# Result weighting, dense stores, result buffers and the pair rate of the last batches in a two-layer graph-attention and mixture-of-experts kernel

## The chip, the cores and the metric

The kernel runs on one core of one Trainium2 chip. The metric is the device time of one execution in microseconds (us), from the first to the last instruction with what lies around it; the median of several runs is compared. TensorE is called PE (its weight loads PEld), VectorE DVE, ScalarE ACT, GpSimd POOL, and SP is the engine that only issues transfers. Each engine works through its own list of instructions in order.

## The reference, cut to what matters

There are 64 batches of 256 tokens with 256 numbers each. Two layers of graph attention and feed-forward work follow each other; the second feed-forward is a mixture of 8 experts, of which each token uses two:

```
x = x + elu(attention of 4 heads over layernorm(x), masked by adj)
x = x + layernorm(x) @ weight.T + bias
x = x + relu(attention of 1 head over layernorm(x), masked by adj)
tokens = layernorm(x)
probs = softmax(tokens @ router_w.T); two largest per token, weights made to sum to 1
out = tokens
for e in range(8):
    h = gelu(tokens @ w1[e] + b1[e]); y = h @ w2[e] + b2[e]
    out = out + combine[:, e] * y
x = x + out
```

## The kernel before

A batch goes through `batch_layers` (L466): four attention heads, the feed-forward layer, one attention head, then the normalised tokens `xng` and the start of the result, `base`. For the first 62 batches `base` is stored to `out` straight away (L563), and the expert part is done by routing. Batches are routed in chunks: 12 chunks of four batches, six of two, two of one. `route` (L860) finds the two experts of each token, works out the row of each in a list in memory, and sends the tokens' rows there with indirect transfers from POOL (`send`, L843).

256 rows of one expert are a **pair** (two blocks of 128). `expert_pair` (L686) loads a pair's rows (`xr`, L701) and its expert's first weights (`we`, L712) from SP's queue, transposes the rows on PE (`px`, L719), copies them on ACT (`sT`, L723), makes the row numbers `to` and the weights `w` on DVE (L726 to L732), multiplies (`ph`, L751), applies gelu on ACT (`hT`, L757), multiplies again (`py`, L766), adds the bias on DVE into a result buffer `y` (L772), and weights `y` by `w` on ACT (L744). `scatter` (L777) then adds the 256 rows to `out` by two indirect transfers with addition from POOL (L783). Every such transfer is made to wait until those of the pair before have landed, so all scatters form one chain. There are 131 pairs, each with two scatter transfers; 14 of them, the partly filled ones, can start only when the last routed batch has been sent.

The last two batches are **dense**: `dense_expert` (L797) runs all eight experts over them, adds into `base` on DVE (L809), and stores `base` at the end (L816) through SP's queue. That gives 16 dense jobs.

The order of all instructions is written by a hand-made scheduler (`while more or active ...`, L1002). Time is cut into *steps*, three steps are a *period*, and a batch starts in each period (at steps 2, 5, 8, ... 191). Every job is a generator; each step runs every active job up to its next `yield`, in the order of the number it yielded before, its *rank*. A low rank comes early in the step. This is the only order there is: an instruction of rank 60 stands behind one of rank 2 in the list of each engine that has both. At the last step of each period pairs are started from a list named `waiting`, as many as a credit allows:

```
if phase == 2:
    credit = min(credit + (2.0 if more else 3.0), 3.0)
    while waiting and credit >= 1.0:
        credit -= 1.0
        begin(waiting.pop(0)(), 90)
```

`more` is true as long as batches are still to be started, up to step 191. A pair that starts at step s issues `xr` at s (rank 90), `we` at s+1 (rank 90), `px`, `sT`, `to` and `w` at s+2 (rank 60), `ph` and `hT` at s+3 (rank 30), `py` and the bias at s+4 (rank 80), and the weighting at s+5 (rank 2). Step s+5 is the same kind of step as s+2, so the weighting of one period's pairs and the row copies `sT` of the next period's pairs are in the same step. Scatters are started one per step at most, at rank 97, from step s+6 on. A dense job issues its `we` load one step, its `ph` three steps and its `py` four steps after it starts; with the eighth job of a batch the store follows at once, ahead of the `we` loads (rank 90) of the same step.

Tiles of one name take turns in a fixed number of buffers: `y` 7, `xr` 5, `we` 7, `z` (the attention probabilities) 6, `me` 2, `to` and `w` 8. PE's outputs share 8 banks.

Of the kernel before, what the change touches and what calls it, by code (L numbers as in the profile page):

```python
# [9 lines left out]
F32 = mybir.dt.float32  # L10
I32 = mybir.dt.int32
# [4 lines left out]
P = 128  # L16
# [11 lines left out]
def kernel(  # L28
# [18 lines left out]
    B, N, D = x.shape  # L47
# [4 lines left out]
    NT = N // P  # L52
# [17 lines left out]
    TICKS = 3  # L70
# [3 lines left out]
    work = ctx.enter_context(tc.tile_pool(name="work", bufs=2))  # L74
# [47 lines left out]
    mhalf = const.tile([P, 2 * NT], F32, tag="mhalf", name="mhalf")  # L122
    nc.vector.memset(mhalf, -0.5)

    adj_i = work.tile([P, NT, N], adj.dtype, tag="z", name="adj_i", bufs=6)
    nc.scalar.dma_start(out=adj_i, in_=adj.rearrange("(t p) j -> p t j", p=P))

    masks = [
# [100 lines left out]


    C_B1, WROW = KT * D, KT * D + 64
    WBUFS, XBUFS, YBUFS = 7, 5, 7
    wpack = tc.dram_tile([E, P, WROW], F32, name="wpack")
    w2s = const.tile([P, E, KT * D], F32, tag="w2s", name="w2s")
    b2s = const.tile([P, E, D], F32, tag="b2s", name="b2s")
# [157 lines left out]
    def projected1(xT, rstd, b):  # L393

        q = q1s[b % 2]
        pqs = []
        for t in range(NT):
            pq = bank("pq", [D + 3])
            for k in range(KT):
                nc.tensor.matmul(  # L400
                    pq, xT[:, k, t * P : (t + 1) * P], wx1[:, k, :],
                    start=(k == 0), stop=(k == KT - 1),
                )
            pqs.append(pq)
        ex = small.tile([P, NT, 3], F32, tag="ex1", name="ex1")
        for t, pq in enumerate(pqs):
            nc.scalar.activation(ex[:, t, :], pq[:, D:], AF.Exp, scale=rstd[:, t : t + 1])
            nc.scalar.activation(
                q[:, t, :D], pq[:, :D], AF.Copy, scale=rstd[:, t : t + 1]
            )  # L410
        me = work.tile([P, NT, N], F32, tag="me", name="me")
        for j in range(NT):
            nc.scalar.activation(me[:, j, :], masks[1][:, j, :], AF.Copy, scale=ex[:, j, 0:1])
        return q, ex, me

    def scores1(ex, me):
        pd = bank("pd", [N])
        for t in range(NT):
            nc.tensor.transpose(
                pd[:, t * P : (t + 1) * P], ex[:, t, 1:2].to_broadcast([P, P]), ident  # L420
            )
        z = work.tile([P, NT, N], F32, tag="z", name="z", bufs=6)
        for j in range(NT):
            nc.vector.scalar_tensor_tensor(
                z[:, j, :], pd, ex[:, j, 2:3], me[:, j, :], op0=ALU.max, op1=ALU.mult
            )
        return z

    def scores(q, heads, hs, mask, probs):

        d = D // heads
        pd = bank("pd", [len(hs), N])
        for i, h in enumerate(hs):
            for t in range(NT):
                nc.tensor.transpose(  # L435
                    pd[:, i, t * P : (t + 1) * P],
                    q[:, t, h, d + 1 : d + 2].to_broadcast([P, P]), ident,
                )
        for i, h in enumerate(hs):
            z = work.tile([P, NT, N], F32, tag="z", name="z", bufs=6)  # L440
            for j in range(NT):
                nc.vector.scalar_tensor_tensor(  # L442
                    z[:, j, :], pd[:, i, :], q[:, j, h, d + 2 : d + 3], mask[:, j, :],
                    op0=ALU.max, op1=ALU.mult,
                )
            probs.append(z)
# [239 lines left out]
    def expert_pair(j, n, ids, ef, regs, needs):  # L686

        i = j % GROUP
        upto = min(j + GROUP, n)
        if i == 0:  # L690
            _, regs["e"] = nc.values_load_multi_w_load_instructions(
                ids[0:1, 0, j:upto], engines=[mybir.EngineType.SP], min_val=0, max_val=E - 1,
                skip_runtime_bounds_check_because=WHY,
            )
            _, regs["t"] = nc.values_load_multi_w_load_instructions(
                ids[0:1, 1, j:upto], engines=[mybir.EngineType.SP], min_val=0, max_val=E * CAP,
                skip_runtime_bounds_check_because=WHY,
            )
        e_sp, t_sp = regs["e"][i], regs["t"][i]
        xr = io.tile([P, 2, ROW], F32, tag="xr", name="xr", bufs=XBUFS)  # L700
        load = nc.sync.dma_start(  # L701
            out=xr,
            in_=xs_d.rearrange("(t p k) c -> t p k c", p=P, k=2)[
                bass.ds(t_sp, 1), :, :, :
            ].rearrange("t p k c -> (t p) k c"),
        )
        tc.add_to_no_dep_group("rows", load.ins)
        for name in needs:
            tc.add_manual_dep(load.ins, name, AFTER, reason="any sent row may lie in the pair")
        yield 90  # L710
        we = io.tile([P, WROW], F32, tag="we", name="we", bufs=WBUFS)
        nc.sync.dma_start(  # L712
            out=we, in_=wpack[bass.ds(e_sp, 1), :, :].rearrange("e p c -> (e p) c")
        )
        yield 60
        px = bank("px", [KT, PAIR])
        for t in range(2):
            for k in range(KT):
                nc.tensor.transpose(  # L719
                    px[:, k, t * P : (t + 1) * P], xr[:, t, k * P : (k + 1) * P], ident  # L720
                )
        xT = work.tile([P, KT, PAIR], F32, tag="sT", name="sT", bufs=3)
        nc.scalar.copy(xT, px)  # L723

        to = small.tile([P, 2], I32, tag="to", name="to", bufs=8)
        nc.vector.tensor_copy(to[:, :, None], xr[:, :, D : D + 1])  # L726
        w = small.tile([P, 2], F32, tag="w", name="w", bufs=8)
        nc.vector.scalar_tensor_tensor(  # L728
            w[:, :, None], xr[:, :, D + 1 : D + 2], ef[:, j : j + 1], xr[:, :, D + 2 : D + 3],
            op0=ALU.is_equal, op1=ALU.mult,  # L730
        )
        nc.vector.tensor_tensor(w[:, :, None], w[:, :, None], xr[:, :, D + 3 : D + 4], ALU.add)  # L732
        yield 30
        hT = hidden(xT, we)
        yield 80
        if i == 0:
            _, regs["x"] = nc.values_load_multi_w_load_instructions(
                ids[0:1, 0, j:upto], engines=[mybir.EngineType.PE, mybir.EngineType.DVE],
                min_val=0, max_val=E - 1, skip_runtime_bounds_check_because=WHY,
            )  # L740
        y = result(hT, bass.ds(regs["x"][i], 1))
        yield 2
        for t in range(2):
            nc.scalar.activation(y[:, t, :], y[:, t, :], AF.Copy, scale=w[:, t : t + 1])  # L744
        scatters.append((y, to))
# [51 lines left out]
    def dense_expert(b, e):  # L797

        own = dense_batch[b]
        yield 90  # L800
        we = io.tile([P, WROW], F32, tag="we", name="we", bufs=WBUFS)
        nc.sync.dma_start(out=we, in_=wpack[e])
        yield 40
        yield 30
        hT = hidden(own["xT"], we)
        yield 80
        y = result(hT, slice(e, e + 1))
        for t in range(NT):
            nc.vector.scalar_tensor_tensor(  # L809
                own["base"][:, t, :], y[:, t, :], own["w"][:, t, e : e + 1],  # L810
                own["base"][:, t, :], op0=ALU.mult, op1=ALU.add,
            )
        if e == E - 1:
            while b == B - 1 and (scatters or len(added) < 2 * PAIRS):
                yield 99
            d = nc.sync.dma_start(  # L816
                out=out_rows[b * N : (b + 1) * N, :].rearrange("(t p) d -> p t d", p=P),
                in_=own["base"],
            )
            before = added[-2:] + based if b == B - 1 else []  # L820
            tc.declare_no_dep(
                d.ins, query=SYNC, group="out", keep=before,
                reason="no row is added to here, or every add is in their chain",
            )
            for ins in before:
                tc.add_manual_dep(d.ins, ins.name, AFTER, reason="filling rows were added here")
            tc.add_to_no_dep_group("out", d.ins)
            nc.sync.nop()
# [168 lines left out]

    batches = jobs()
    step, more, credit = 2, True, 0.0
    SETUP_AT = 3  # L1000
    with tc.manual_schedule():
        while more or active or waiting or dense_jobs or scatters:  # L1002
# [6 lines left out]
            if step >= SETUP_AT and setup:  # L1009
                begin(setup.pop(0)(), 90)  # L1010
            if phase == 2:
                credit = min(credit + (2.0 if more else 3.0), 3.0)
                while waiting and credit >= 1.0:
                    credit -= 1.0
                    begin(waiting.pop(0)(), 90)
                for _ in range(2):
                    if dense_jobs:
                        begin(dense_jobs.pop(0)(), 90)
# [54 lines left out]
```

## Time and profile before

| What | Value |
|---|---|
| Median of 3 runs | 1713.54 us (1712.98 to 1722.15) |
| The profiled execution: its own time | 1715.78 us |
| Its span, first to last instruction | 1714.1 us |
| PE busy | 1550.8 us, 90% of the span |
| DVE busy | 1276.3 us, 74% |
| ACT busy | 897.4 us, 52% |
| POOL busy | 875.9 us, 51% |
| Mean granted PE clock | 0.958 of full |

A line of the profile's fifth part gives: source line, engine, operation, output and inputs, count, busy time and mean of one in ns, and then the idle time of the engine just before these instructions with what ended most of it. In a timeline a line gives start, duration, engine, line, and in square brackets the idle time before it. POOL's time for an indirect transfer is that of issuing it; when it has landed is seen from what waits for it.

### The profile page before, as it was taken

How to read it: one execution, taken by the hardware profiler on the slowest of the kernel's cores; microseconds unless marked ns; L12 is line 12 of the kernel's file. 1: busy time of each engine (PE TensorE's matmuls, PEld its weight loads, DVE VectorE, ACT ScalarE, POOL GpSimd, SP SyncE). 2: the span in 40 equal slices, each digit the busy share in tenths (PEclk: the TensorE clock that was granted, in tenths of full speed). 3: DMA queues.
4: the chain of work that ended last, by engine and by line, in shares of the span. 5: the costliest groups of instructions: out<-in, count | busy, mean ns of one | idle time of the engine just before them, and what ended most of it. 6: DMA issues, size and time to landing. Idle time of an engine off the chain costs nothing. (4 is left out here: it accounts for less than half of the span.)

```text
span 1714.1 us, 29732 instructions
## 1 busy us (share of the span) xinstructions
PE 1550.8 (90%) x8998; PEld 1366.5 (80%) x8998; DVE 1276.3 (74%) x4744; ACT 897.4 (52%) x1965; POOL 875.9 (51%) x790
## 2 busy tenths in 40 slices
PE   5899889899999999999999999999999998797792
PEld 4777778788888888898888888888889887676681
DVE  5889998978787888878787878788788977522221
ACT  0243435366656665666666555666556665533240
POOL 0121334436566565646565656565674656634444
PEclk8999899899999999999999999999999999899896
DMA  4812223245656465656555455556464556674653
GB/s 101 222 46 56 60 76 84 62 128 129 152 125 152 110 142 112 143 125 145 132 134 133 101 137 121 144 128 151 108 143 115 116 138 144 169 195 97 146 129 43
DMA packets 272541, 209.67 MB, mean 122 GB/s; under 512 B 153848, under 2 KB 226560, under 8 KB 272384
## 3 DMA queue, kind: packets, MB, share of 16 engines
q1 hardware_dynamic: 221760, 139.40, 29.8%
q0 software_dynamic: 49632, 67.39, 21.6%
q8 instruction: 74, 1.21, 0.3%
q10 hardware_dynamic: 992, 0.99, 0.2%
q14 instruction: 83, 0.68, 0.1%
HBM read 118.55 MB, written 89.15 MB: 121 GB/s over the span
## 5 line engine op out<-in xcount | busy, mean ns | idle before, releaser
L783 POOL DMA_INDIRECT out_dram<-y,to x262 | 417.9, 1595 | 322.5 <-DMA out_dram<-y,to 161.2
L456 PE MATMUL pv<-q,z 128*128 128x65 f32 (+1 forms) x2560 | 377.2, 302 | 7.0 <-DVE z L442 3.6
L456 PEld LDWEIGHTS pv<-q,z 128*128 128x128 f32 x2560 | 338.0, 197 | 21.0 <-DVE z L442 4.4
L751 PE MATMUL ph<-sT,we 128*128 128x256 f32 x1048 | 250.4, 395 | 45.2 <-ACT sT L723 23.7
L843 POOL DMA_INDIRECT xs<-xng,pos x248 | 252.0, 1016 | 69.2 <-issue 66.9
L344 POOL TENSOR_SCALAR rstd<-mv 128x4 f32<-128x4 f32 (+1 forms) x132 | 65.4, 496 | 428.2 <-DVE mv L337 340.6
L751 PEld LDWEIGHTS ph<-sT,we 128*128 128x128 f32 x1048 | 203.1, 199 | 76.7 <-ACT sT L723 25.1
L766 PE MATMUL py<-w2s,hT 128*128 (+1 forms) x1176 | 263.7, 379 | 0.0
L766 PEld LDWEIGHTS py<-w2s,hT 128*128 128x128 f32 x1176 | 219.6, 190 | 27.8
L355 ACT COPY xT<-pt 128x512 f32<-128x512 f32 x192 | 113.0, 588 | 232.9 <-PE pt L351 210.7
L772 DVE TENSOR_TENSOR y<-py,b2s 128x512 f32<-128x512 f32 x147 | 97.7, 688 | 165.2 <-PE py L766 108.0
L442 DVE SCALAR_TENSOR_TENSOR z<-pd,q,mask 128x256 f32<-128x256 f32 x512 | 210.9, 473 | 5.7 <-PE pd L435 3.2
L757 ACT ACTIVATE hT<-ph,we 128x256 f32<-128x256 f32 x294 | 123.2, 470 | 157.0 <-PE ph L751 113.4
L744 ACT ACTIVATE y<-y,w 128x256 f32<-128x256 f32 x262 | 113.1, 501 | 121.9 <-DVE y L772 118.8
L345 POOL TENSOR_TENSOR rstd<-rstd,mhalf 128x4 f32<-128x4 f32 (+1 forms) x132 | 157.2, 1191 | 11.0
L336 DVE BATCH_NORM_STATS2 stats<-x 128x6 f32<-128x256 f32 x384 | 156.3, 407 | 2.2
L365 PE MATMUL pq<-wx,xT 128*128 128x268 f32 x512 | 139.1, 418 | 8.2 <-DVE wt L239 4.2
L400 PE MATMUL pq<-wx,xT 128*128 128x259 f32 x512 | 129.2, 394 | 16.1 <-ACT xT L355 13.8
L365 PEld LDWEIGHTS pq<-wx,xT 128*128 128x128 f32 x512 | 103.2, 205 | 30.9 <-issue 7.6
L400 PEld LDWEIGHTS pq<-wx,xT 128*128 128x128 f32 x512 | 91.9, 189 | 42.8 <-ACT xT L355 26.8
L511 PE MATMUL pf<-wfT,xT 128*128 128x256 f32 x512 | 123.7, 385 | 0.0
L533 ACT ACTIVATE rel<-pv,rinv 128x256 f32<-128x256 f32 x128 | 53.8, 472 | 120.5 <-DVE rinv L463 105.0
(155 smaller groups left out, 2400.9 us busy)
## 6 DMA issues: line engine op xcount, KB each, us to landing
we<-wpack SPq DMA_DIRECT2D x147, 288.0 KB
xr<-xs SPq DMA_DIRECT2D x131, 260.0 KB
xblk<-in_x_dram SPq DMA_DIRECT2D x256, 64.0 KB
xin<-in_x_dram SPq DMA_DIRECT2D x64, 256.0 KB
out_dram<-base SPq DMA_DIRECT2D x64, 256.0 KB
out_dram<-y,to POOLq DMA_INDIRECT x262
xs<-xng,pos POOLq DMA_INDIRECT x248
xs<-fill SPq DMA_DIRECT2D x9, 260.0 KB
```

Source lines behind the costliest of these rows:

```text
L336: nc.vector.bn_stats(stats[:, t, :], src[:, t, :])
L345: nc.gpsimd.tensor_tensor(rstd[:, :n], rstd[:, :n], mhalf[:, :n], ALU.pow)
L365: nc.tensor.matmul(pq.rearrange("p h c -> p (h c)"), xT[:, k, t * P : (t + 1) * P], wx[:, k, :], start=(k == 0), stop=(k == KT - 1),)
L400: nc.tensor.matmul(pq, xT[:, k, t * P : (t + 1) * P], wx1[:, k, :], start=(k == 0), stop=(k == KT - 1),)
L442: nc.vector.scalar_tensor_tensor(z[:, j, :], pd[:, i, :], q[:, j, h, d + 2 : d + 3], mask[:, j, :], op0=ALU.max, op1=ALU.mult,)
L456: nc.tensor.matmul(pv[:, h, :], z[:, j, t * P : (t + 1) * P], q[:, j, h, : d + 1], start=(j == 0), stop=(j == NT - 1),)
L511: nc.tensor.matmul(pf[:, t, :], xT[:, k, t * P : (t + 1) * P], wfT[:, k, :], start=(k == 0), stop=(k == KT - 1),)
L751: nc.tensor.matmul(ph[:, f, :], we[:, k * D + f * P : k * D + (f + 1) * P], xT[:, k, :], start=(k == 0), stop=(k == KT - 1),)
L757: nc.scalar.activation(hT[:, f, :], ph[:, f, :], AF.Gelu, bias=we[:, C_B1 + f : C_B1 + f + 1])
L766: nc.tensor.matmul(py[:, t, :], hT[:, f, t * P : (t + 1) * P], w2s[:, e, f * D : (f + 1) * D].rearrange("p e c -> p (e c)"), start=(f == 0 ...
L783: d = nc.gpsimd.indirect_dma_start(out=out_rows, out_offset=bass.IndirectOffsetOnAxis(ap=to[:, t : t + 1], axis=0), in_=y[:, t, :], in_off ...
L843: d = nc.gpsimd.indirect_dma_start(out=xs_d[: E * CAP * PAIR, :], out_offset=bass.IndirectOffsetOnAxis(ap=at, axis=0), in_=xe, in_offset=None,
```

## The change

Seven edits of five kinds.

1. In `expert_pair` the weighting of `y` keeps its step but moves from rank 2 to rank 65, behind the copies `sT` of the next pairs' rows (rank 60).
2. In `dense_expert` the eighth job of a batch yields once more, at rank 99, before it issues the store of `base`. The store so comes one step later.
3. `y` gets 8 buffers instead of 7; `to` and `w` get 12 instead of 8.
4. Room for these is taken from `z` (5 buffers instead of 6) and `me` (1 instead of 2).
5. The credit grows by 3 a period from step `DRAIN_AT` = 144 on (the last 16 batches), and no longer only after the last batch has started.

```diff
-    adj_i = work.tile([P, NT, N], adj.dtype, tag="z", name="adj_i", bufs=6)
+    adj_i = work.tile([P, NT, N], adj.dtype, tag="z", name="adj_i", bufs=5)
...
-    WBUFS, XBUFS, YBUFS = 7, 5, 7
+    WBUFS, XBUFS, YBUFS = 7, 5, 8
...
-        me = work.tile([P, NT, N], F32, tag="me", name="me")
+        me = work.tile([P, NT, N], F32, tag="me", name="me", bufs=1)
...
-        z = work.tile([P, NT, N], F32, tag="z", name="z", bufs=6)
+        z = work.tile([P, NT, N], F32, tag="z", name="z", bufs=5)
...
-            z = work.tile([P, NT, N], F32, tag="z", name="z", bufs=6)
+            z = work.tile([P, NT, N], F32, tag="z", name="z", bufs=5)
...
-        to = small.tile([P, 2], I32, tag="to", name="to", bufs=8)
+        to = small.tile([P, 2], I32, tag="to", name="to", bufs=12)
...
-        w = small.tile([P, 2], F32, tag="w", name="w", bufs=8)
+        w = small.tile([P, 2], F32, tag="w", name="w", bufs=12)
...
         y = result(hT, bass.ds(regs["x"][i], 1))
-        yield 2
+        yield 65
         for t in range(2):
             nc.scalar.activation(y[:, t, :], y[:, t, :], AF.Copy, scale=w[:, t : t + 1])
...
         if e == E - 1:
+            yield 99
             while b == B - 1 and (scatters or len(added) < 2 * PAIRS):
                 yield 99
             d = nc.sync.dma_start(
...
     step, more, credit = 2, True, 0.0
+    DRAIN_AT = TICKS * (B - 16)
...
-                credit = min(credit + (2.0 if more else 3.0), 3.0)
+                credit = min(credit + (2.0 if step < DRAIN_AT else 3.0), 3.0)
```

## The prediction

> **What bounds the kernel now.** I read first the busy times by stretch (columns: span, then busy time of PE, PEld, DVE, ACT, POOL with counts, PE clock, share of the transfer engines, GB/s).
>
> ```profile
> 1290.00:1380.00 90.00, 89.05 (x549) 80.19 (x548) 80.96 (x327) 56.05 (x122) 53.18 (x48) 1.00 0.47 105
> ...
> 1430.00:1490.00 60.00, 45.66 (x220) 39.57 (x219) 35.13 (x209) 32.61 (x66) 41.84 (x36) 0.86 0.60 142
> ...
> 1530.00:1605.00 75.00, 52.84 (x251) 45.92 (x250) 19.16 (x58) 22.76 (x52) 32.82 (x21) 0.89 0.56 116
> ...
> 1660.00:1714.00 54.00, 20.50 (x101) 17.73 (x99) 9.46 (x24) 8.76 (x20) 24.28 (x16) 0.73 0.36 44
> ```
>
> Up to about 1420 us PE is 95 to 99% busy: the body is PE's. After that no engine is full, so something else sets the pace. PE's timeline there shows what PE waits for:
>
> ```profile
> 1480.21 6.93 PE L751 MATMUL ph<-sT,we 128*128 128x256 f32 x24 [7.28 <-ACT sT L723]
> ...
> 1551.36 7.19 PE L751 MATMUL ph<-sT,we 128*128 128x256 f32 x24 [8.66 <-ACT sT L723]
> ...
> 1604.29 8.01 PE L751 MATMUL ph<-sT,we 128*128 128x256 f32 x24 [12.54 <-DMA we<-wpack]
> ```
>
> The row copies `sT` come late because ACT first weights `y`, and that waits for DVE's `y`, which waits for a buffer. The 12.54 us is SP's queue: the store L816 (issued at 1599.95) holds the `we` loads behind it. These are the waits that the change attacks. But are they the path? POOL's timeline says no:
>
> ```profile
> 1628.90 1.55 POOL L783 DMA_INDIRECT out_dram<-y,to  x1 [3.11 <-ACT hT L757]
> 1630.76 1.55 POOL L783 DMA_INDIRECT out_dram<-y,to  x1 [0.30 <-issue]
> 1638.02 1.55 POOL L783 DMA_INDIRECT out_dram<-y,to  x1 [5.71 <-ACT y L744]
> ...
> 1697.68 1.55 POOL L783 DMA_INDIRECT out_dram<-y,to  x1 [3.03 <-DMA out_dram<-y,to]
> 1699.54 1.55 POOL L783 DMA_INDIRECT out_dram<-y,to  x1 [0.31 <-issue]
> 1704.07 1.55 POOL L783 DMA_INDIRECT out_dram<-y,to  x1 [2.97 <-DMA out_dram<-y,to]
> 1705.92 1.55 POOL L783 DMA_INDIRECT out_dram<-y,to  x1 [0.30 <-issue]
> ```
>
> Two lines are one pair. At the end a pair follows a pair every 6.4 us (1697.68 to 1704.07), with nothing between them but the landing of the one before. Counting pairs back from the last (131st at 1704.07), the 105th starts at 1522.05: 26 links in 182.0 us, 7.0 each. In all this time the chain never runs dry. The three pairs multiplied at 1513.9 had their first `y` weighted at 1517, and are scattered from 1543; those of 1615.6 are ready at 1619 and go at 1629. So every PE wait of the drain is covered by 10 to 26 us of queued scatters. The end is **the number of scatters still to do when the body is over, times their pace**, plus 10.0 us after the last start. From 1419 to 1488 POOL is full too: sends, norms and scatters follow each other with only the chain's landings between.
>
> **What the Trainium skill says.** "DMA: Bandwidth & Descriptors", rules for kernel authors: an accumulating transfer must wait for the semaphore of any earlier one on the same bytes. That is why this chain is serial; the trace agrees (6.4 us, never less, from pair to pair). Same page, on issuing engines not being separate queues: all transfers share the same engines and interleave. The trace agrees: with `we` and `xr` loads under way the links take 8.3, 8.3 and 8.05 us (from 1597.45) instead of 6.4. "Perfetto Trace Analysis", SWDGE instruction: the recorded end is that of making descriptors, not of landing; here 1.55 us recorded, some 3.8 us more to landing in the chain of waits. "TensorE: Matmul & The Clock Gate", what is actually happening: after an idle window the clock drops. Here 24 `ph` matmuls take 5.34 to 5.45 us, and 6.93 to 8.45 after the long waits.
>
> **Which pairs move.** Counting the scheduler's loop by hand gives pairs started per period, before to after. Until step 143 nothing differs. In the four-batch cycles, 3,2,2,1 becomes 3,3,2,0 three times (the last pair of steps 152, 164, 176 starts early; sum unchanged). At steps 182, 185, 188, 191 the list holds 7 to 12 pairs, and 2 becomes 3: four pairs earlier. At 206 the list is nearly empty and 3 becomes 1; the last period (230) has 1 instead of 3. Since a pair is scattered six steps after its start, one per step, 30 scatters were left after step 208 and 26 will be: **four links fewer in the drain**.
>
> **The sum, part by part.** A period's length is read from one start of L365 to the next on PE: 26.5 to 27.2 us with three pairs, 22.1 or 22.5 with two, 19.1 with one, 15.6 with none (107 to 154 us, where few sends run).
>
> 1. Four pairs more in full body periods: 4 x (26.6 - 22.35) = **+17 us**. Nothing is given back at step 206: until then POOL, not PE, sets the pace.
> 2. Three periods without pairs. A third pair adds 4.3; dropping the only pair saves 19.1 - 15.6 = 3.5 at best, but DVE's busy time in the one-pair period at 961 is 17.96, which without a pair's own parts (0.69 for `y`, 0.5 for `to` and `w`) is 16.8, so 2.3 at worst. Each costs 0.8 to 2.0; I take 1.4: **+4 us**.
> 3. Weighting at rank 65. In one-pair periods DVE waits 0.55 us for ACT's `q` (L373), which stands behind the weighting; POOL's norm is ready 0.55 us earlier, and PE then waits 0.6 to 0.9 for DVE's `by`. Eight such periods remain: 8 x 0.55 = **-4 us** (0 to -8). In the others PE waits 0.24 for an `xT`, untouched. The weighting itself comes 2 to 4 us later; its scatter stands a step later and, from 1425 on, a pair is scattered 13 us or more after its weighting: that hides it. Now queued behind it are `e`'s exponential and `hT`: 1.7 us later, while `e` in the period at 870 us is ready some 4 us before its reader. In the drain the PE waits of 2.5, 3.4, 7.3, 8.7 and 1.0 us shrink; worth nothing while the scatter chain covers them. If the cover went, they and their slow clock would be some 20 us.
> 4. The store a step later: the `we` loads (3 + 2) pass it and the 12.5 us wait goes; behind it now stand the next `xr` loads, read two steps later. Hidden by the same chain: 0. The last store already waits for all scatters: 0.
> 5. Eight `y` buffers: one scatter more of slack in DVE's `y` (45.1 us of waiting). Hidden by the chain: 0. `to` and `w`: DVE's one wait of 8.8 us goes, also under the chain: 0. Bound of both: 0 to -9.
> 6. `z` and `me`. The fifth `z` back was last read by the attention matmuls that stand on PE ahead of the transposes `pd` which the new `z` needs anyway; `me` is rewritten two steps after its reader. The wait is implied by one that exists: 0. If not, at most DVE's gap of 1 us in 64 batches; I exclude more because `pd` is ordered on PE.
> 7. Four links fewer: 4 x 7.0 = **-28 us** (6.43 without loads: -26). PE can't replace the chain as the bound: seven periods of 18.7 us and one of 10.9 end 142 us after the first drain `ph`, while the chain, starting 25 us after it, needs 22 x 6.43 = 141 more.
> 8. A third scatter per period on POOL in the seven periods that grow: 3.8 us of issuing. POOL in the cycle at 1100 us waits 9.9 and 5.65 us for DVE's `mv`, which covers it: 0, upper bound below.
>
> Sum: 17 + 4 - 4 - 28 = **-11 us**: span 1714.1 to 1703, execution 1715.8 to 1705. The median of the runs is 2.2 us under the profiled execution, so **1703 us**.
>
> **Rivals.** *POOL becomes the bound (slower).* In each of the seven periods POOL has three scatters (11.3 us issuing), four to six sends at 1.28, two norms (3.4), and up to 3.2 us of landing before each scatter (9.6): 29.4 to 32 against 26.6. It decides from where the idle time before the norm L344 is gone: then ACT's `q`, DVE and PE wait for the norm behind the scatter. Taking 4 us each: +28, sum +17, 1730 us. For it: ACT's `q` already waits 65.1 us for POOL's norms. Against it: the landing waits overlap sends and norms in most periods.
>
> *PE's waits count after all.* If POOL is full between 1430 and 1490 only because it waits for late `y`, the three `sT` waits (13.2 us) and part of the slow clock come off the path: -17 more, 1686 us. For it: two scatter waits there are put down to ACT's `y`. Against: by count their pairs were weighted a period before.
>
> *Moved work is paid back in full.* Links at 6.43 and dearer empty periods, and no gain at the norms: 17 + 6 - 26 = -3, or the queue never holds more pairs than the old credit took: 1711 to 1714.
>
> **How the numbers follow.** About 0.5% (8.6 us) is what a measurement of this kernel can tell from no change. Forecast 0.42, its own terms spread about 8 us, so 0.25 of it is faster by more than that and 0.17 within; PE's waits 0.20, faster; paid back 0.22, of which 0.19 within, 0.01 faster, 0.02 slower; POOL 0.16, of which 0.15 slower and 0.01 within. Faster 0.46, within 0.37, slower 0.17. The range goes from the second rival to halfway between forecast and slow rival and beyond the paid-back case: 1686 to 1720.
>
> **What would show it.** Right: 26 scatters after the last send, still 6.4 to 8 us apart and never waiting for `y`; body periods of 3,3,2,0 pairs of 26.6, 26.6, 22.4 and about 16.5 us; last PE work earlier but the chain still ending last; no 12 us wait for `we`. Wrong: norms that wait behind scatters in the periods from 1290 us on, scatters that wait for ACT in the drain, or a drain of 30 links.

## The result: slower, and the profile after

The changed kernel takes 1733.7 us (median of 4 runs, 1733.1 to 1736.3) against 1713.3. The ratio is 1.0134, with a 95% interval from 1.0108 to 1.0160: slower by 20 us in the medians, by 23 us (18 to 27) by the ratio, where 10 us faster was forecast. The profiled execution has a span of 1731.4 us.

The busy times by stretch show two things (same columns as before; the stretches follow the same work, which now lies later).

```profile
1048.00:1068.00 20.00, 17.76 (x108) 14.89 (x107) 19.07 (x73) 8.70 (x22) 13.33 (x12) 1.00 0.48 80
1068.00:1105.00 37.00, 30.69 (x154) 26.53 (x154) 20.44 (x67) 18.65 (x42) 20.36 (x19) 0.82 0.65 167
1300.00:1390.00 90.00, 89.05 (x529) 79.75 (x528) 75.85 (x306) 55.69 (x123) 44.61 (x40) 1.00 0.48 121
...
1550.00:1650.00 100.00, 100.00 (x484) 87.88 (x483) 31.65 (x90) 41.42 (x100) 42.17 (x27) 0.98 0.71 171
1690.00:1731.00 41.00, 2.69 (x13) 2.02 (x11) 3.16 (x7) 0.91 (x2) 18.20 (x12) 0.58 0.36 45
```

The drain (the time after the last send, when only pairs and dense jobs are left) is what the edits aimed at: from 1550 to 1650 us PE is busy without a gap, where before it had 52.84 of 75 us. But it still ends with scatters alone, 41 us with 2.69 us of PE. And in the body there is something new, the second line: a stretch of 37 us in which PE is busy 30.69 and its clock falls to 0.82. It is the period that follows one without pairs. Reading a period's length again from one start of L365 to the next on PE:

| Pairs in the period, before | us | Pairs, after | us |
|---|---|---|---|
| 3 | 28.4 | 3 | 26.3 |
| 2 | 22.1 | 3 | 26.0 |
| 2 | 22.5 | 2 | 22.5 |
| 1 | 19.1 | 0 | **17.3** |
| 3, the next cycle's first | 26.9 | 3 | **37.2** |

The empty period takes 17.3 us (16.9 and 19.6 in the other two cycles) where about 16.5 was forecast. The one after it is 10 us too long, and so it goes three times (37.2, 37.2, 37.8 us). PE's timeline of the first one, and PE's list of waits for the whole run (total us, times, longest), say what it waits for; the list of the kernel before has no such line:

```profile
1056.63 1.99 PE L511 MATMUL pf<-wfT,xT 128*128 128x256 f32 x8
...
1067.84 2.96 PE L365 MATMUL pq<-wx,xT 128*128 128x268 f32 x8
...
1083.30 3.78 PE L511 MATMUL pf<-wfT,xT 128*128 128x256 f32 x8 [5.67 <-DVE q L381]
```

```profile
PE pf L511 <- DVE q L381: 18.1, 3, 6.6
```

The eight L511 matmuls take 3.78 us after the wait instead of 1.99 in the period before it: slow matmuls come on top of the wait. DVE's `q` waits 10.40 us for ACT's `q` there, and ACT's for a norm:

```profile
1082.45 0.43 ACT L373 ACTIVATE q<-pq,rstd 128x12 f32<-128x12 f32 x2 [9.49 <-POOL rstd L345]
```

And this is why POOL's norm is late (POOL's timeline, every instruction of the stretch):

```profile
1065.75 1.10 POOL L844 DMA_INDIRECT xs<-xng,pos  x1 [0.20 <-issue]
1067.15 0.98 POOL L844 DMA_INDIRECT xs<-xng,pos  x1 [0.30 <-issue]
1068.43 1.62 POOL L783 DMA_INDIRECT out_dram<-y,to  x1 [0.30 <-issue]
1070.36 1.57 POOL L783 DMA_INDIRECT out_dram<-y,to  x1 [0.30 <-ACT me L413]
1072.23 1.00 POOL L844 DMA_INDIRECT xs<-xng,pos  x1 [0.30 <-issue]
1073.53 0.99 POOL L844 DMA_INDIRECT xs<-xng,pos  x1 [0.30 <-issue]
1077.55 1.60 POOL L783 DMA_INDIRECT out_dram<-y,to  x1 [3.03 <-DMA out_dram<-y,to]
1079.45 1.55 POOL L783 DMA_INDIRECT out_dram<-y,to  x1 [0.30 <-issue]
1080.49 0.81 POOL L344 TENSOR_SCALAR rstd<-mv 128x4 f32<-128x4 f32 x1
1081.38 1.04 POOL L345 TENSOR_TENSOR rstd<-rstd,mhalf 128x4 f32<-128x4 f32 x1
```

From 1065.75 to 1080.49 POOL issues four sends and two pairs' scatters, with one 3.03 us wait for a landing among them, and only then comes the norm L344. It has no idle time in front of it: its last input had been there for 8.9 us, as DVE's timeline shows.

```profile
1071.40 0.18 DVE L337 BATCH_NORM_AGGREGATE mv<-stats 128x2 f32<-128x6 f32 x1
```

In the kernel before only one scatter stands between the same two norms:

```profile
1066.37 0.57 POOL L344 TENSOR_SCALAR rstd<-mv 128x4 f32<-128x4 f32 x1 [1.18 <-DVE mv L337]
...
1073.98 1.61 POOL L783 DMA_INDIRECT out_dram<-y,to  x1 [0.30 <-ACT q L408]
1075.89 1.58 POOL L783 DMA_INDIRECT out_dram<-y,to  x1 [0.30 <-issue]
1076.92 0.83 POOL L344 TENSOR_SCALAR rstd<-mv 128x4 f32<-128x4 f32 x1
```

There the two norms start 10.6 us apart (1066.37 and 1076.92), in the change 17.1 us apart (1063.35 and 1080.49). A period without pairs is light for PE, but not for POOL: in its three steps (154 to 156 here) stand three scatters instead of two, of the third pair that step 146 now starts and of both pairs of step 149. POOL comes to these steps when PE is at their end (1065.75, where PE's period runs from 1050.51 to 1067.84). PE went through the period in 17 us; POOL could not.

At the other end the forecast held. After the last send 27 pairs are scattered (26 had been counted, and 30 for the 31 of the kernel before), the first starting at 1533.3 and the last here (POOL's timeline):

```profile
1715.00 1.55 POOL L783 DMA_INDIRECT out_dram<-y,to  x1 [3.00 <-DMA out_dram<-y,to]
...
1721.17 1.55 POOL L783 DMA_INDIRECT out_dram<-y,to  x1 [2.75 <-DMA out_dram<-y,to]
```

That is 187.9 us for 26 links, where before it was 216.2 us for 30 (1487.8 to 1704.1): 28.3 us less. But this chain starts 45.4 us later than before: the last batch's L365 starts 34.1 us later (1392.3 instead of 1358.2), and from there to the last send it takes 11.3 us longer.

### The profile page after: what moved, and what is told of

It reads as the page before. It is cut to its first block, busy times and chain, and to the rows that moved or that the text cites. A ratio compares the mean times of both kernels' runs of the same rounds, so it can differ in the third digit from the quotient of the medians.

```text
span 1731.4 us, 29722 instructions
## 1 busy us (share of the span) xinstructions
PE 1562.7 (90%) x8998; PEld 1374.0 (79%) x8998; DVE 1276.1 (74%) x4744; ACT 886.3 (51%) x1959; POOL 871.6 (50%) x790
## 5 line engine op out<-in xcount | busy, mean ns | idle before, releaser
L456 PEld LDWEIGHTS pv<-q,z 128*128 128x128 f32 x2560 | 337.1, 196 | 19.6 <-DVE z L442 5.2
L344 POOL TENSOR_SCALAR rstd<-mv 128x4 f32<-128x4 f32 (+1 forms) x132 | 62.9, 477 | 468.3 <-DVE mv L337 387.8
L511 PE MATMUL pf<-wfT,xT 128*128 128x256 f32 x512 | 131.5, 403 | 18.2 <-DVE q L381 18.1
L365 PE MATMUL pq<-wx,xT 128*128 128x268 f32 x512 | 138.2, 416 | 8.7 <-DVE wt L239 4.2
L373 ACT ACTIVATE q<-pq,rstd 128x12 f32<-128x12 f32 x128 | 30.1, 271 | 188.7 <-POOL rstd L345 160.7
L365 PEld LDWEIGHTS pq<-wx,xT 128*128 128x128 f32 x512 | 101.7, 202 | 31.3 <-issue 7.6
L511 PEld LDWEIGHTS pf<-wfT,xT 128*128 128x128 f32 x512 | 98.8, 203 | 31.6 <-DVE q L381 19.1
```

What stands on the lines that cost most here:

```text
L365: nc.tensor.matmul(pq.rearrange("p h c -> p (h c)"), xT[:, k, t * P : (t + 1) * P], wx[:, k, :], start=(k == 0), stop=(k == KT - 1),)
L456: nc.tensor.matmul(pv[:, h, :], z[:, j, t * P : (t + 1) * P], q[:, j, h, : d + 1], start=(j == 0), stop=(j == NT - 1),)
L511: nc.tensor.matmul(pf[:, t, :], xT[:, k, t * P : (t + 1) * P], wfT[:, k, :], start=(k == 0), stop=(k == KT - 1),)
```

## The experiments

Theory A after this result: **POOL falls behind where a period passes faster than POOL's queued scatters, sends and norms, and the norm behind them then holds ACT, DVE and PE.** Theory B: a third scatter in a period holds the norms wherever it stands. Theory C: the other edits cost the time. Ratios are against the kernel before, run on the same chip at the same time (its medians lie between 1706.9 and 1713.5 us from one set of runs to another, so ratios are compared, not times); intervals are of 95%.

### One part undone, or done alone

**The rate undone**, all other edits kept:

```diff
-                credit = min(credit + (2.0 if step < DRAIN_AT else 3.0), 3.0)
+                credit = min(credit + (2.0 if more else 3.0), 3.0)
```

> The change with its credit edit undone; rank 65, the later store and all buffer edits stay. Theory A (each period without pairs passes faster than POOL can work off the scatters, sends and norms that are queued; the next period waits for a norm): no period is empty, so the 27 us lost there are gone; the drain has 30 scatters again and is as long as before; only the 4 us gained in the one-pair periods stay: about 1709 us. Theory B (a third scatter a period holds the norms, wherever it is): also about 1709. Theory C (the weighting's new rank, or one z and one me fewer, cost the time): above 1720, since all of these are still in.

Measured: 1706.5 us, ratio 0.9975 (0.9960 to 0.9990). The other edits together are worth some 4 us of gain (2 to 7); theory C falls.

**The rate alone**, put into the kernel before (the edit above the other way round, and the line that sets `DRAIN_AT` to 144):

> The kernel before with the credit edit alone. Theory A and B: the loss is all here; 27 us in three empty periods, some 17 us for four more pairs in full periods, 28 us won in the drain, and 0 to 7 us between: 1729 to 1737 us, the periods after the empty ones 35 us or longer instead of 27. Theory C: within 5 us of the kernel before.

Measured: 1737.7 us, ratio 1.0145 (1.0111 to 1.0178). The periods after the empty ones take 37.4, 37.2 and 37.6 us. The whole loss is in this one line. The time is just above the 1729 to 1737 us expected.

**The rate from step 180** on, in the changed kernel:

```diff
-    DRAIN_AT = TICKS * (B - 16)
+    DRAIN_AT = TICKS * (B - 4)
```

> The whole change, but three pairs a period only from step 180 (the last 4 batches): no period is empty, the same four pairs still start early, and 26 scatters are left for the drain as in the change. Theory A: the change less its 27 us, about 1706 us. Theory B: the periods from 182 to 191 still have the third scatter and hold the norms: above 1718. Theory C: near 1733.

Measured: 1705.3 us, ratio 0.9954 (0.9941 to 0.9968), as theory A has it. The periods with three pairs after step 180 take 26.0 and 26.4 us, and PE has no wait in them above 0.24 us. That alone doesn't settle theory B, since the scatters of these pairs come two periods later: 12 transfers fall in the three periods, and 11 did in the kernel before. But in every cycle of the kernel before three scatters stand in one period (steps 149 to 151, for example), and the periods there take 22.1 and 22.5 us; so "wherever it stands" is too much. Between this run and the change (0.9954 to 1.0134) lie 1.8%, or 31 us, and the edit differs only in the three cycles with an empty period. The two traces agree: from the first L365 of step 143's batch to that of step 182's they differ by 30.3 us.

**The weighting's rank alone**, in the kernel before:

```diff
-        yield 2
+        yield 65
         for t in range(2):
             nc.scalar.activation(y[:, t, :], y[:, t, :], AF.Copy, scale=w[:, t : t + 1])
```

> The kernel before with the weighting at rank 65 as its only edit. The prediction's third step: the one-pair periods lose DVE's wait of 0.55 us for ACT, eleven of them, and in the drain the scatter chain covers the rest: 4 to 6 us faster than before. Rival (PE's waits in the drain count): 12 us faster or more. Rival (the gain of the run with the rate undone came from the buffers or the store): within 2 us of before.

Measured: 1711.8 us, ratio 0.9987 (0.9973 to 1.0001). A gain of some 2 us is likeliest, less than the 4 to 6 expected, and none is not excluded. In the drain PE's waits for `sT` vanish, 9.6 us before; the time does not follow them:

```profile
PE ph L751 <- ACT sT L723: 9.6, 2, 8.7
```

This is the kernel before from 1490 us on; with the rank alone the list of PE's waits has no such line.

**The store alone**, in the kernel before:

```diff
         if e == E - 1:
+            yield 99
             while b == B - 1 and (scatters or len(added) < 2 * PAIRS):
```

> The kernel before with the dense store one step later as its only edit. The prediction's fourth step: the wait of 12.5 us for we goes from PE's timeline, the scatter chain still ends last, and the time stays within 2 us of before. Rival (PE's wait was on the path): 8 to 12 us faster.

Measured: 1714.9 us, ratio 1.0004 (0.9984 to 1.0024). PE's waits in the drain, from the list of waits (total us, times, longest): before, then with the store later.

```profile
PE ph L751 <- DMA we<-wpack: 20.1, 2, 12.5
```

```profile
PE ph L751 <- ACT sT L723: 17.8, 5, 6.6
PE ph L751 <- DMA we<-wpack: 8.6, 1, 8.6
```

The 12.5 us wait is gone and the waits for `sT` have grown from 9.6 to 17.8: what PE no longer waits for the weights, it waits in part for the scatters in another place. In the same stretch DVE's `y`, for which ACT's weighting and the row copies behind it wait, waits 75.2 us for scatters to land instead of 44.9.

**The buffers alone** (y 8, `to` and `w` 12, z 5, me 1, as in the diff of the change), in the kernel before:

> The kernel before with the buffer edits alone (y 8, to and w 12, z 5, me 1). The prediction's steps 5 and 6: within 2 us of before. Rival (the 2 us that the run with the rate undone is faster than the weighting's rank alone come from here): 2 to 4 us faster. Rival (a z or me fewer holds DVE or ACT): 2 us slower or more.

Measured: 1709.1 us, ratio 1.0005 (0.9988 to 1.0022). Nothing in either direction that this can tell. Added up, the three single runs give less than 1 us of gain, with some 5 us of uncertainty either way; whether the 4 us of the run with the rate undone are more than their sum stays open, since the intervals overlap.

### POOL's load taken away, and moved

**Half the scatters in the three cycles.** In the changed kernel, one of the two transfers of each pair is left out:

```diff
+        cut = 152 <= order_steps[-1] < 182
-        for t in range(2):
+        for t in range(1 if cut else 2):
...
```

> The whole change, but of the pairs scattered in steps 152 to 181 only the first 128 of 256 rows are added to the result; the second transfer is left out, all other work stays. POOL's issuing for these scatters is halved. Theory A and B: the norms are no longer held, the three periods after the empty ones fall from 37 us to 27 to 29 us, in all 20 to 28 us: about 1709 us. Rival D (an empty period is bad in itself: DVE's route work or a cold PE clock makes the next one long): they stay above 34 us and the time falls by less than 6.

Measured: 1704.5 us, ratio 0.9954 (0.9938 to 0.9970), 1.8% or some 31 us below the change. The periods after the empty ones take 28.4, 29.1 and 28.5 us, while the empty ones still take 16 to 17. An empty period is not bad in itself: rival D falls. The edit takes away the transfers as well as POOL's issuing of them; the next run keeps both.

**The same scatters, three steps later.** This one leaves nothing out:

```diff
-            if scatters:
+            held = 153 < step < 181 and (step - 154) % 12 < 3
+            if scatters and not held:
```

> The whole change, all its work done, but no scatter is issued in the three steps of each empty period (154 to 156, 166 to 168, 178 to 180); they follow in the next three steps, which had none. 26 scatters are left for the drain as in the change. Theory A (POOL's queued scatters hold the norm behind the empty period): the periods after the empty ones fall from 37 us to 27 to 30 us and the time by 18 to 28 us, to 1706 to 1716 us. Rival (the scatters hold the norms wherever they stand, since POOL has the same amount to do): the next periods stay above 33 us and the time above 1724.

Measured: 1706.9 us, ratio 1.0007 (0.9989 to 1.0025), 1.3% below the change. The periods after the empty ones take 27.5, 27.9 and 28.9 us. POOL's timeline at the place shown above:

```profile
1067.31 0.96 POOL L844 DMA_INDIRECT xs<-xng,pos  x1 [0.30 <-issue]
1068.57 0.96 POOL L844 DMA_INDIRECT xs<-xng,pos  x1 [0.30 <-issue]
1070.55 0.23 POOL L344 TENSOR_SCALAR rstd<-mv 128x4 f32<-128x4 f32 x1 [1.02 <-DVE mv L337]
```

The norm starts at 1070.55 instead of 1080.49, and again POOL waits for it and not it for POOL. With the same work on every engine, the place of some scatters in POOL's list is worth about 22 us (16 to 27). That shows theory A as directly as it can be shown here, and theory B falls: the moved scatters make three in the period they move to, and the period that PE runs next takes 26.0 us. Why the ratio stays 0.5% above that of the rate from 180 is open; the two runs were on different chips, and their profiled spans (1704.8 and 1705.9 us) do not show it.

**Half the scatters of steps 185 to 208**, in the kernel with the rate from 180 (the same edit with other steps):

> The change with the rate from step 180, and of the pairs scattered in steps 185 to 208 only the first 128 of 256 rows are added to the result; the rest of the work stays. It asks what made the way from the last full period to the last send 8 us longer than four pairs explain. If it is POOL (theory A, here at work a second time): the last send comes 8 to 18 us earlier than in the run with the rate from 180, and the end with it: 1687 to 1697 us. If it is DVE's route work or PE: the last send moves by less than 3 us, the end too.

Measured: 1686.3 us, ratio 0.9824 (0.9791 to 0.9857), and in the profile the way from the start of L365 of the last batch to the last send takes 116 us instead of 142 (and 128 in the kernel before). The last send itself comes 17 us earlier than in the run with the rate from 180, within the 8 to 18 named; measured from that start it is 26 us, and the ratio says 1.3% or 22 us. It is POOL's scatters again; in this stretch, which holds 28 sends as well, the scatters of periods with three pairs do cost time. This edit too takes away transfers together with their issuing, and which of the two counts more was not separated.

**Half the scatters of the drain**, in the same kernel:

> The change with the rate from step 180, and of the 26 pairs scattered from step 209 on only the first 128 of 256 rows are added to the result. If the chain of scatters is the bound of the drain: a link takes some 4.6 us instead of 7.2, PE becomes the bound (142 us from its first drain ph), and the end comes 20 to 28 us earlier: 1677 to 1685 us. If PE, ACT or SP set the drain's pace: less than 6 us earlier.

Measured: 1679.9 us, ratio 0.9787 (0.9755 to 0.9820), 1.7% or some 28 us less. Now PE's end stands close to the kernel's end:

```profile
1663.91 5.34 PE L766 MATMUL py<-w2s,hT 128*128 x24
```

It is the last line of PE's timeline in a span of 1679.7 us: PE ends 10 us before the end, where in the run with the rate from 180 it ended 42 us before it (1663.9 of 1705.9). The chain was the drain's bound. The links that are left take 6.1 us in the mean and not the 4.6 expected, and half of the waits between them are put down to ACT's `y` or `hT`: the chain now often waits for its pairs.

### Even periods

**Two pairs in each period, three from step 179**, with all other edits of the change:

```diff
-    DRAIN_AT = TICKS * (B - 16)
+    DRAIN_AT = TICKS * (B - 4) - 1
...
-                credit = min(credit + (2.0 if step < DRAIN_AT else 3.0), 3.0)
+                rate = 2.0 if step < DRAIN_AT else 3.0
+                credit = min(credit + rate, rate)
```

> The whole change with another rule of credit: exactly two pairs a period up to step 178, with no saving up, and three from step 179 on. No period has one or no pair; 26 scatters are left for the drain. Theory A, carried on (a period takes as long as its slowest engine, so an uneven load costs wherever one engine runs out): a cycle of 3,2,2,1 takes 26.9 + 22.1 + 22.5 + 19.1 = 90.6 us, one of 2,2,2,2 some 89.3; 1.3 us less in ten cycles, 13 us less than the run with the rate from 180: about 1692 us. Rival (PE bounds all these periods alike, so their order is worth nothing): within 4 us of 1705.

Measured: 1698.1 us, ratio 0.9934 (0.9911 to 0.9958). **The lowest ratio of this study** among the kernels that do all the work: some 11 us faster than the kernel before and 2.0% faster than the change. Against the run with the rate from 180 it is 0.2% (some 3.5 us) better, not the 13 us expected, and since the intervals overlap a difference from it is not shown.

**The same rule alone**, in the kernel before (`rate` is 2 as long as `more` is true, and 3 after that):

> The kernel before with two pairs a period and no saving up while batches start, as its only edit; 30 or 31 scatters are left for the drain. Theory A: 1.3 us in eleven cycles, some 14 us faster than before, about 1699 us. Rival: within 4 us of before.

Measured: 1704.6 us, ratio 0.9974 (0.9961 to 0.9987), 4 us of gain (2 to 7) instead of 14. In its profile the body does become shorter: the last batch's L365 starts at 1340.7 us instead of 1358.2, and most periods take 22.1 to 22.8 us each. But its drain has one link more, since no credit is saved up for step 179, and both kernels with this rule lose part of it again in two periods of 28 to 30 us near 1193 to 1250 (PE waiting 2.9 us for `z`, and short stops put down to issue), where the sends of the first chunks of two batches set in: 10 or 11 sends fall in the first of the two, against 4 in a usual one. What exactly collides there was not tried.

## Why the prediction was wrong

The error is nearly all in one step, the second.

1. *Four pairs more in full periods, +17 us.* Held for those periods: 26.0 to 26.4 us with three pairs, 3.9 more than with two. But the step went on: nothing is given back at 206 because POOL sets the pace there. That was right and I did not price it: if POOL sets the pace from 1419 us on, the scatters that these steps bring forward have to be paid there too. Between the last batch's L365 and the last send 17 pairs are scattered instead of 13.5. This way grew from 128.3 to 139.7 us in the change, 7 more than the fourth pair explains, and taking half of the scatters away shortens it to 116.
2. *Three periods without pairs, +4 us.* **This is the step that failed.** It took the period's length from PE (15.6) and DVE (16.8) and left out the third engine. POOL's list for those three steps holds three scatters (11.3 us of issuing), four to six sends at 1.28 and two norms (3.4): 20 to 22 us of issuing alone against a period of 17. These prices stood in the prediction, in the rival. Measured: the empty period is 17.3, but the next is 37.2 instead of 26.9; the three cycles cost about 31 us in all (the change against the rate from 180), not 4. The 15.6 us came from 107 to 154 us, before the first scatter (305 us); the prediction noted that few sends run there and did not ask what that meant. The norm was not free of the scatters before, either: at 1076.92 us it starts with no idle time in front of it, 2.3 us after its last input. PE did not feel it, so the sign that the rival names was already there, unread.
3. *Rank 65, -4 us.* Right in its place: one-pair periods fall from 19.1 to about 18.6 us. In the total -2 (0 to -5) alone.
4. *The store, 0*, and 5, *the buffers, 0*, and 6, *z and me, 0*: right as far as can be told, 1.0004 and 1.0005 with some 3 us of uncertainty each. The trace of the store alone fits the reason that was given: the wait is gone, others grow, and the end does not move.
7. *Four links fewer, -28 us.* Right: 28.3 us. (The least distance from pair to pair in the kernel before is 6.27 us, so the prediction's "6.4 us, never less" is a little too strong; and its 3.8 us to landing count from the start of an issue, with the 1.55 us in them: the chain's last wait ends at 1703.3 us, and the transfer had started at 1699.54.)
8. *A third scatter on POOL, 0.* Wrong for the reason of step 2. The cover that it names, POOL's idle 9.9 and 5.65 us for `mv`, belongs to periods of 22 to 28 us. Around the empty period it is 2.07 and 1.63 us, and nothing before the late norm.

Put together: the forecast of -11 us, 27 more for step 2 and 7 more for step 1 give +23, which is what the ratio shows.

The slower rival, at 1730 us, had the right mechanism, the norm behind the scatters, and nearly the right time, but it was put in the seven periods that gain a pair. Those take 26.0 to 26.4 us, nothing extra. That its time came out is luck: it took 4 us in each of seven periods, and it was some 10 us in each of three. The place was one or two periods later, because a pair's scatter comes six steps, two periods, after its start. I had counted that delay for the drain and not for the empty periods.

The rival that PE's waits count after all fell with the store alone and the rank alone, where a wait goes and the time does not follow. Its reason, that POOL is full there only because it waits for late `y`, fell with half the scatters of steps 185 to 208: with less of POOL's own work the stretch is 26 us shorter.

## What to carry to other kernels

When work is moved from one period to another, write down the load of every engine in every period, each at the delay at which that engine meets the work: a period that is empty for the matmul engine can be the fullest one for the engine that finishes the results two periods later. Small operations that others wait for, here norms of 128x4, should not stand in one in-order list behind long issue-and-wait work; if they must, keep that work spread as evenly as the shortest period allows. And a wait of the busiest engine is worth nothing while a serial chain behind it has work queued: count the links left and their pace first.

## What the runs showed that I had not expected

- Moving scatters by three steps in POOL's list, with no work changed, was worth some 22 us of 1734.
- The first period with the 5.7 us wait on PE was 10 us too long: the rest is mostly slow matmuls, before the wait (L365 in 2.96 us instead of 1.97) and after it (L511 in 3.78 instead of 1.99). Those before it follow a gap of 1.72 us; in the run with the moved scatters L365 takes 2.04 us after a gap of 1.71, so the gap alone does not decide it.
- POOL's list bounds more of this kernel than its 50% of busy time lets one think. Leaving out half of the scatters of 24 steps near the end gave 1.3%, or 22 us (0.9954 to 0.9824).
